# A fill on GpSimd behind every gather of token rows in an embedding and MLP kernel

## Chip, cores and metric

The kernel runs on one core of a Trainium2 chip. The metric is the device time of one execution in microseconds (us); the median of three runs is given, with the lowest and the highest. A profile is one further execution, recorded by the hardware profiler.

The engines are called as in the profile: PE is TensorE (PEld its weight loads), DVE is VectorE, ACT is ScalarE, POOL is GpSimd, and SP is the engine that issues the plain DMAs.

## Reference

A recommendation model over 16384 rows. Every row has 32 token indices into a table of 50000 x 300, three lists of 20 indices into tables of 1000, 5000 and 10000 rows of 64, and four single indices into small tables. The lists are averaged, everything is concatenated to 748 columns, and an MLP of three layers follows. A "wide" sum of one scalar per looked-up index is added before the sigmoid.

```python
tok = word_emb[token_idx].mean(axis=1)                 # (B, 32) -> (B, 300)
e1 = emb_mh1[mh1_idx].mean(axis=1)                     # (B, 20) -> (B, 64); e2, e3 alike
o1 = emb_oh1[oh1_idx]                                  # (B,) -> (B, 64); o2, o3, o4 alike
emb = jnp.concatenate([tok, e1, e2, e3, o1, o2, o3, o4], axis=1)
wide = (wide_mh1[mh1_idx].sum(axis=(1, 2)) + ... + wide_oh4[oh4_idx][:, 0])[:, None]
h = jax.nn.relu(emb @ W1 + b1)                         # 1024
h = jax.nn.relu(h @ W2 + b2)                           # 512
h = jax.nn.relu(h @ W3 + b3)                           # 256
return jax.nn.sigmoid(h @ Wd + bd + wide)
```

## The kernel before

The 16384 rows are cut into 128 tiles of 128 rows. Four tiles make a block for the MLP (the last block is cut into 2, 1 and 1 tiles). Two kinds of lookup run side by side.

**The small tables** are held on the chip, split into three bf16 terms (`terms`). For a tile, one-hot rows are made on VectorE (`one_hots`, L280), TensorE multiplies them into counts (`counts`, L298), ScalarE copies the counts out of PSUM as fp8 (L305), and TensorE multiplies counts by `terms` to get the sums of embeddings (`small_sums`, L323), which VectorE reduces into the tile's row of features `g` (L330).

**The token rows** come from memory. `tokens` walks over the 32 tokens of a tile in 16 groups of two. For each group it takes a buffer `tok_rows` of 128 x 600 floats from a pool of six (`2 * TOK_LAG`), and GpSimd issues two indirect DMAs (L212), each of which fetches one row of 300 floats for each of the 128 partitions. There are 128 x 32 = 4096 such gathers in all. The group is then put on a list, `under_way`. Only when more than three groups are on it (`TOK_LAG`) is the oldest added up by VectorE in `add_up`: the two halves of the buffer into each other (L202), and that into `g` (L203); the first group of a tile goes straight into `g` (L200). A buffer is free for a new gather once L203 (or L200) has read it.

The order on every engine is the order in which the program is written out by hand (`manual_schedule`). The main loop takes each tile in 11 steps. A step issues the one-hots of the next step, the counts of this one, some groups of gathers and additions, some of the small sums of the tile before, and some matmuls of the MLP of the block before. The last three are generators under `Paced`, which hands out their work evenly: 16 token groups over the 11 steps of a tile, so one or two groups in a step. In VectorE's queue, the additions of a step stand behind its one-hots and ahead of those of the following step.

The MLP runs in fp32 on TensorE (L376), with ScalarE applying bias and ReLU (L385). Features are transposed on TensorE (L366) and scaled into `x` by VectorE (L367).

GpSimd has nothing to do but the gathers, apart from seven small instructions at the start: four fills of one column (L518), a fill of 128 x 128 floats for the identity matrix (masks.py:197), a select on it, and an iota.

Of the kernel before, what the change touches and what calls it, by code (L numbers as in the profile page):

```python
# [8 lines left out]
F32 = mybir.dt.float32  # L9
# [8 lines left out]
P = 128  # L18
# [3 lines left out]
D1, D2, D3 = 1024, 512, 256  # L22
TOK_GROUP = 2
TOK_LAG = 3
BLOCK = 512
HALF = P // 2
N_SMALL = 3 * N_MH + 4
# [17 lines left out]
def kernel(  # L45
# [21 lines left out]
    nc = tc.nc  # L67
    B = out.shape[0]
    NSUB = BLOCK // P
    M1, M2, M3 = D1 // P, D2 // P, D3 // P  # L70
# [9 lines left out]

    tokp = ctx.enter_context(tc.tile_pool(name="tok", bufs=2 * TOK_LAG))
    const = ctx.enter_context(tc.tile_pool(name="const", bufs=1))
# [110 lines left out]
            nc.sync.dma_start(out=sb, in_=dram)  # L193

    under_way = []

    def add_up(rows, g, first):
        a, b, n = rows[:, 0:TOK_D], rows[:, TOK_D : 2 * TOK_D], TOK_D
        if first:
            nc.vector.tensor_add(g[:, 0:n], a, b)  # L200
        else:
            nc.vector.tensor_add(a, a, b)  # L202
            nc.vector.tensor_add(g[:, 0:n], g[:, 0:n], a)  # L203

    def tokens(g, it):


        for q in range(N_TOK // TOK_GROUP):
            rows = tokp.tile([P, TOK_GROUP * TOK_D], F32, name="tok_rows")
            for t in range(TOK_GROUP):  # L210
                j = q * TOK_GROUP + t
                nc.gpsimd.indirect_dma_start(  # L212
                    out=rows[:, t * TOK_D : (t + 1) * TOK_D],
                    out_offset=None,
                    in_=word,
                    in_offset=bass.IndirectOffsetOnAxis(ap=it[:, j : j + 1], axis=0),
                )
            under_way.append((rows, g, q))
            if len(under_way) > TOK_LAG:
                rows, to, old_q = under_way.pop(0)  # L220
                add_up(rows, to, old_q == 0)
            yield 1
# [5 lines left out]
    def load_indices(blk):  # L228


        b0 = blk * BLOCK
        it = idxp.tile([P, NSUB, N_TOK], I32, name="it")
        nc.sync.dma_start(
            out=it, in_=idx[b0 : b0 + BLOCK, 0:N_TOK].rearrange("(s p) c -> p s c", p=P)
        )
# [122 lines left out]
    def transposed(gs):  # L358

        n = len(gs) * P  # L360
        x = xp.tile([P, NK, BLOCK], F32, name="x", tag="even")
        for k in range(NK):
            kk = chunk_k[k]
            pt = ps_h.tile([P, BLOCK], F32, name="pt", tag="ph")
            for s, g in enumerate(gs):
# [6 lines left out]
    def layer(dst, weights, bias, src, kks, n_out, n):  # L372
        for m in range(n_out):
            ph = ps_h.tile([P, BLOCK], F32, name="ph", tag="ph")
            for k, kk in enumerate(kks):
# [68 lines left out]
    for t in range(tiles + 1):  # L444
# [4 lines left out]
        if t < tiles:  # L449
            if s == 0 and t:  # L450
                it, sc = next_it, next_sc
            g = gp.tile([P, G_COLS], F32, name="g")
            cnt = cp.tile([P, 2, HALF, n_h], FP8, name="cnt", tag="counts")
            toks = Paced(tokens(g, it[:, s, :].bitcast(U32)), N_TOK // TOK_GROUP, STEPS)
        else:
            last_tokens()
# [76 lines left out]
```

## Time and profile before

| | |
|---|---|
| runs | 5517.34 us median of 3 (5515.67 to 5519.1) |
| profiled execution | 7368.99 us, its span 7367.2 us |
| mean granted TensorE clock, profiled execution | 0.891 |
| PE busy | 5894.3 us (80% of the span) |
| POOL busy | 4079.8 us (55%) |
| DVE busy | 3606.2 us (49%) |
| ACT busy | 2632.3 us (36%) |
| gathers L212 | 4096 of 996 ns |
| DMA, share of 16 engines | 31.1% for the gathers, 629.41 MB |

The busy times belong to the profiled execution and are shares of its span, which is 1.34 times the median of the runs. A busy time counts the records of instructions alone: time in which an engine prepares its next instruction is not in it, and appears as idle time with the releaser "issue". Where a wait is listed, the line reads: engine and line that waited, arrow, engine and line that ended the wait, then us in total, times, and the longest in us. In a timeline, a line reads: start in us, duration in us, engine, line, operation, output and inputs, and in brackets the idle time before it and what ended that.

### The profile page before, as it was taken

What the parts mean: (1) busy time and instruction counts of PE and PEld (TensorE: products, weight loads), DVE (VectorE), ACT (ScalarE), POOL (GpSimd) and SP (SyncE); (2) the same over time, 40 slices, a digit from 0 to 9 for tenths busy, and PEclk for the clock granted to TensorE, in tenths of its full rate; (3) what the DMA queues carried; (4) which work ended last, traced back from release to release, by engine and by line L of the source; (5) the groups of instructions that cost most, each with busy time, mean ns of one, the idle gap of its engine ahead of it and who ended that gap; (6) DMA issues with size and microseconds to landing.
All of it is one profiled execution on the core that took longest, in us unless ns stands there. A gap on an engine that the chain in (4) does not pass through costs nothing.

```text
span 7367.2 us, 103052 instructions
## 1 busy us (share of the span) xinstructions
PE 5894.3 (80%) x41320; PEld 3527.7 (48%) x41320; DVE 3606.2 (49%) x8013; ACT 2632.3 (36%) x3408; POOL 4079.8 (55%) x4103
## 2 busy tenths in 40 slices
PE   3688788878778888878888888888888788888789
PEld 2444444444444444444444444444444444444457
DVE  5544454445454454445444544454445454545443
ACT  4333333333333333333333333333333333333333
POOL 5555555555555555555555555555555555555552
PEclk8789888899898998889888889888988898888999
DMA  5333333333333333333333333333333333333331
GB/s 138 89 90 91 87 87 88 87 90 85 89 86 90 90 88 90 86 89 86 93 86 88 87 90 91 87 87 89 89 89 89 86 90 90 86 91 87 90 87 45
DMA packets 245345, 652.52 MB, mean 89 GB/s; under 512 B 108978, under 2 KB 111989, under 8 KB 244864
## 3 DMA queue, kind: packets, MB, share of 16 engines
q0 software_dynamic: 196608, 629.41, 31.1%
q1 hardware_dynamic: 48255, 16.53, 1.0%
q8 instruction: 323, 5.29, 0.3%
q14 instruction: 159, 1.29, 0.1%
HBM read 645.59 MB, written 0.07 MB: 88 GB/s over the span
## 4 chain that ended last, share of the span: by engine, by line
PE 52%; another core or an unknown queue 26%; ACT 13%; issue 5%; DVE 3%; POOL 0%; DMA 0%; DVEq 0%; SPq 0%; ACTq 0%; POOLq 0%
PE ph L376 24%; PE pg L323 17%; ACT cnt L305 12%; PE pc L298 9%; ACT h L385 1%; PE pt L366 1%; DVE x L367 1%; PE po L399 1%; DVE g L330 0%; PE po L403 0%; DVE slice L280 0%; DVE tok_rows L202 0%; DVE g L203 0%; ACT terms L166 0%
## 5 line engine op out<-in xcount | busy, mean ns | idle before, releaser
L212 POOL DMA_INDIRECT tok_rows<-in_word_emb_dram,it x4096 | 4078.9, 996 | 3207.7 <-DVE g L203 2195.9
L305 ACT ACTIVATE cnt<-pc 128x828 fp8e3<-128x828 f32 (+1 forms) x2816 | 2224.6, 842 | 3325.2 <-PE pc L298 1393.4
L323 PE MATMUL pg<-terms,cnt 128*128 128x195 bf16 x17664 | 2135.3, 271 | 272.0 <-issue 257.2
L280 DVE TENSOR_TENSOR row<-iota,sc 128x768 bf16<-128x768 bf16 (+1 forms) x1408 | 764.7, 543 | 2673.5 <-remote 1282.8
L323 PEld LDWEIGHTS <-cnt 128*128 128x128 fp8e3 x17664 | 1759.2, 147 | 502.7 <-issue 363.6
L298 PE MATMUL pc<-slice,row 64*128 64x138 bf16 x16384 | 880.2, 232 | 1047.6 <-ACT cnt L305 883.0
L376 PE MATMUL ph<-x,w_sb 128*128 128x512 f32 (+5 forms) x3264 | 1625.2, 626 | 43.7 <-issue 41.5
L298 PEld LDWEIGHTS <-row 64*128 64x128 bf16 x16384 | 570.1, 97 | 2182.3 <-issue 1611.2
L376 PE MATMUL ph<-h,w_sb 128*128 128x512 f32 (+2 forms) x2720 | 1404.9, 645 | 26.5 <-issue 24.7
L203 DVE TENSOR_TENSOR g<-g,tok_rows 128x300 f32<-128x300 f32 x1920 | 904.6, 471 | 65.6
L202 DVE TENSOR_TENSOR tok_rows<-tok_rows 128x300 f32<-128x300 f32 x1920 | 890.4, 464 | 0.0
L376 PEld LDWEIGHTS ph<-x,w_sb 128*128 128x128 f32 (+1 forms) x3264 | 610.5, 211 | 516.7 <-issue 505.3
L280 DVE TENSOR_TENSOR slice<-iota,sc 128x828 bf16<-128x828 bf16 (+1 forms) x1408 | 803.8, 571 | 0.0
L385 ACT ACTIVATE h<-ph,b_sb 128x512 f32<-128x512 f32 (+2 forms) x476 | 315.4, 663 | 1225.4 <-remote 739.8
L376 PEld LDWEIGHTS ph<-h,w_sb 128*128 128x128 f32 x2720 | 524.4, 217 | 422.9 <-issue 420.5
L330 DVE TENSOR_REDUCE g<-pg 128x130 f32<-128x390 f32 (+1 forms) x512 | 249.8, 509 | 827.9 <-remote 392.0
L367 DVE TENSOR_SCALAR x<-pt,scale 128x512 f32<-128x512 f32 (+4 forms) x204 | 140.9, 717 | 111.1 <-PE pt L366 104.4
L366 PE MATMUL pt<-ident,g 128*128 128x128 f32 (+1 forms) x768 | 124.8, 292 | 51.8 <-DVE x L367 51.4
L366 PEld LDWEIGHTS pt<-ident,g 128*128 128x128 f32 (+1 forms) x768 | 84.5, 143 | 91.7 <-DVE x L367 83.8
L305 ACT ACT_TABLE_LOAD x32 | 41.1, 1283 | 145.8 <-PE pc L298 145.0
L399 PE MATMUL po<-h,wd_sb 128*1 128x512 f32 (+2 forms) x136 | 62.0, 573 | 0.6 <-issue 0.3
L200 DVE TENSOR_TENSOR g<-tok_rows 128x300 f32<-128x300 f32 x128 | 59.2, 463 | 0.0
(32 smaller groups left out, 346.4 us busy)
## 6 DMA issues: line engine op xcount, KB each, us to landing
tok_rows<-in_word_emb_dram,it POOLq DMA_INDIRECT x4096
ix<-in_idx_dram SPq DMA_DIRECT2D x128, 32.0 KB
w_sb<-in_W_dram SPq DMA_DIRECT2D x6, 512.0 KB
it<-in_idx_dram SPq DMA_DIRECT2D x32, 64.0 KB
w_sb<-in_W_dram SPq DMA_DIRECT2D x1, 2048.0 KB
raw<-in_mh_dram SPq DMA_DIRECT2D x1, 975.0 KB
out_dram<-h SPq DMA_DIRECT2D x31, 2.0 KB
raw<-in_mh_dram SPq DMA_DIRECT2D x1, 292.5 KB
```

Source lines behind the costliest of these rows:

```text
L202: nc.vector.tensor_add(a, a, b)
L203: nc.vector.tensor_add(g[:, 0:n], g[:, 0:n], a)
L212: nc.gpsimd.indirect_dma_start(out=rows[:, t * TOK_D : (t + 1) * TOK_D], out_offset=None, in_=word, in_offset=bass.IndirectOffsetOnAxis(ap ...
L280: nc.vector.tensor_tensor(one[:, 0:rows, :].rearrange("p i (n d) -> p i n d", d=2), iota[:, 0:n].rearrange("p (n d) -> p n d", d=2).unsque ...
L298: nc.tensor.matmul(pc[:, f, k * n_h : (k + 1) * n_h], hot[0][half, k0 + k, :], hot[1][half, k0 + k, :], start=True, stop=True,)
L305: nc.scalar.activation(cnt[:, :, b + k0 : b + k0 + n, :].rearrange("l f k h -> l f (k h)"), pc[:, :, 0 : n * n_h], AF.Copy, scale=0.5, sat ...
L323: nc.tensor.matmul(pg[:, j, :], by_slice[:, :, h], terms[:, h, :], start=(h == h0), stop=(h == h1 - 1))
L330: nc.vector.tensor_reduce(g[:, at : at + n * ROW].rearrange("p (f d) -> p f d", f=n), pg[:, 0:n, :].rearrange("p f (c d) -> p f d c", c=3) ...
L366: nc.tensor.transpose(pt[:kk, s * P : (s + 1) * P], chunk(g, k), ident)
L367: nc.vector.tensor_scalar(x[:kk, k, 0:n], pt[:kk, 0:n], scale[:kk, k : k + 1], None, ALU.mult)
L376: nc.tensor.matmul(ph[:, 0:n], weights[:kk, k, m * P : (m + 1) * P], src[:kk, k, 0:n], start=(k == 0), stop=(k == len(kks) - 1),)
L385: nc.scalar.activation(dst[:, m, 0:n], ph[:, 0:n], AF.Relu, bias=bias[:, m : m + 1])
```

## The change

A tile `pause` of 128 x 128 floats is added, and after each gather GpSimd fills it with zeros. Nothing reads `pause`. There are 4096 fills, all in GpSimd's own queue.

```diff
+PAUSE = 128
...
     under_way = []
+    pause = const.tile([P, PAUSE], F32, name="pause")
...
     def tokens(g, it):
...
                     in_=word,
                     in_offset=bass.IndirectOffsetOnAxis(ap=it[:, j : j + 1], axis=0),
                 )
+                nc.gpsimd.memset(pause, 0.0)
             under_way.append((rows, g, q))
```

## Prediction

> **What bounds the kernel now.** I read the times first, then the page's chain (part 4), then the waits, then GpSimd's own groups and timeline. The runs take 5517.34 us (median of three, 5515.67 to 5519.1); the profiled execution took 7368.99, a span of 7367.2 with 1.8 around it. It is a third slower than the runs, so I ask first what it has that they may lack. The chain answers:
>
> ```profile
> PE 52%; another core or an unknown queue 26%; ACT 13%; issue 5%; DVE 3%; POOL 0%; DMA 0%; DVEq 0%; SPq 0%; ACTq 0%; POOLq 0%
> ```
>
> A kernel on one core has no other core to wait for. Listed in order of time, these pieces are stalls of mostly 9.2 us, 26.2% in all (26% above): 0.262 x 7367.2 = 1930 us. Without them 5437 us are left, close to the runs. I take the stalls for the recording's, and the runs for an execution with few of them. That is an inference.
>
> POOL (GpSimd) has 0% of the chain, and the waits make it look idle:
>
> ```profile
> POOL tok_rows L212 <- DVE g L203: 2195.9, 1064, 9.8
> ...
> POOL tok_rows L212 <- issue: 876.6, 2827, 2.1
> ```
>
> A gather waits until the addition of L203 frees its buffer, 2195.9 us in all; nobody in the list waits for gathered rows. Read alone, this says that GpSimd has room. But the second line is no slack: 876.6 / 2827 = 0.31 us is lost ahead of gathers that waited for nothing. The timeline of POOL, where gathers run unhindered, shows the same:
>
> ```profile
> 2001.87 0.95 POOL L212 DMA_INDIRECT tok_rows<-in_word_emb_dram,it  x1 [0.30 <-DVE g L203]
> 2003.12 0.95 POOL L212 DMA_INDIRECT tok_rows<-in_word_emb_dram,it  x1 [0.30 <-issue]
> 2004.37 0.95 POOL L212 DMA_INDIRECT tok_rows<-in_word_emb_dram,it  x1 [0.30 <-issue]
> 2005.63 0.95 POOL L212 DMA_INDIRECT tok_rows<-in_word_emb_dram,it  x1 [0.30 <-issue]
> ```
>
> Starts are 1.25 us apart, not 0.95: each gather costs its record plus 0.30. The first line shows that 0.30 also when DVE is named as releaser. The groups of POOL, shapes apart:
>
> ```profile
> L212 POOL DMA_INDIRECT tok_rows<-in_word_emb_dram,it x4096 | 4078.9, 996 | 3207.7 <-DVE g L203 2195.9 <-issue 876.6 <-DVE g L200 64.8
> ...
> masks.py:197 POOL MEMSET ident<- 128x128 f32 x1 | 0.2, 205 | 0.3 <-POOLq L518 0.3
> ...
> L518 POOL MEMSET const-float32-0.0<- 128x1 f32 x1 | 0.1, 99 | 0.2 <-issue 0.2
> ```
>
> The mean gather is 0.996 us; with a gap of 0.305 (between the 0.30 and the 0.31 above) GpSimd needs 1.301 us per gather and 4096 x 1.301 = 5329 us. Gathers begin 3.0 us into the span and the last starts at 7287.1, 80 before its end: 5329 + 83 = 5412 us is the least that GpSimd allows. In the profiled execution that is 73% of the span; in the runs it would be 98%. TensorE stands as near: 5894.3 us busy at a mean granted clock of 0.891 is 5252 us at full clock. **Two engines, both a few per cent under 5517**: that is my reading.
>
> **What the Trainium skill says.** "Perfetto Trace Analysis", section GPSIMD Engine Instruction, calls GpSimd's recorded spans unreliable and would have one time by the spacing of starts; the trace agrees (0.95 recorded, 1.25 apart). "GPSIMD Engine Reference", 3.1, gives 1.03 cycles per element at 1.2 GHz for simple bodies, 110 ns for 128 columns by my estimate; the trace agrees (205 - 99 = 106 ns between the two fills above). The same page, 2.1, says that one GpSimd instruction doesn't hold the next back until it has completed; the trace agrees for fills, since four one-column ones at the start begin about 28 ns apart (0.25, 0.28, 0.30, 0.33 us) while each records 99 to 119 ns. "SBUF — State Buffer", Who interferes with whom, says that a VectorE operation with two inputs in SBUF contends with GpSimd instructions that read SBUF, not with those that only write it; no row here shows a fill beside VectorE.
>
> **The change part by part.** Nothing is removed and nothing moved; no DMA and no queue on SP is touched. 4096 fills are added to GpSimd's queue, one after each gather, all to one tile that nobody reads, so no other engine waits for a fill. Behind a fill stand the next gather of the pair, and the next pair.
>
> - *One fill.* The same operation on the same shape (128x128 f32) records 205 ns: one price, if the next gather starts only when the fill has been written. The other is its throughput, 28 ns of issue + 106 ns for the columns = 134 ns, if the write's tail overlaps what follows. I take the middle, 0.17 us. The outer ends are 0 (it fits inside the 0.305 us between gathers) and 0.51 (205 ns plus a second gap of 0.305).
> - *The sum on GpSimd.* 4096 x 0.17 = 696 us. 4096 x (1.301 + 0.17) = 6025, and with 83 at the ends **6108 us**. With 0.134 it is 5961, with 0.205 it is 6252.
> - *What covers it.* In the profiled execution, the 2195.9 us of waits for L203; there 6108 still fits under 7367.2, and I expect its span to grow little, to between 7370 and 7600. In the runs the cover is only 5517 - 5412 = 105 us, or 0.026 us per gather; of 696 us, 591 stick out.
> - *What is late next.* `add_up` stands in VectorE's queue ahead of the next step's one-hots (L280). When gathered rows come late, L200 or L202 waits for the DMA, L280 behind them, then the count matmuls (L298), ScalarE's copies (L305) and the other matmuls behind those on TensorE. The six buffers let GpSimd run some groups ahead, which smooths bursts but adds nothing to a rate that is too low everywhere: a tile of 128 rows takes 5517 / 128 = 43.1 us now and would need 32 x 1.471 = 47.1 us of GpSimd.
> - *The extra tile* takes 512 bytes per partition of SBUF: no time.
>
> **Rivals.**
> 1. *The fill is hidden* (not slower). If the 0.305 us between gathers is preparation of the next gather, and the fill runs meanwhile, it costs up to 0.026 us and the bound isn't reached: 5517, within a few us. For it: the gap is constant and nothing that the profile shows fills it. Against it: the gap may be spent by the very cores that would run the fill. It decides below (5517 - 83) / 4096 - 1.301 = 0.026 us per fill. A slight gain is possible if spaced gathers disturb others less.
> 2. *The gather is shorter in the runs than in the profile.* The record's minimum spacing is 1.245; with 1.25 and 0.134 the sum is 4096 x 1.384 + 83 = 5752. For it: the recording lengthens other things. Against it: a denser execution has VectorE busier, and gathers beside VectorE's additions last 1.12 us and not 0.95 (2000.45, while L202 runs).
> 3. *A fill breaks the gathers apart* and brings a dispatch gap of its own: 0.51 us, 4096 x 1.811 + 83 = 7501. For it: the gap stands before every gather. Against it: the small fills at the start have none between them. Half of that extra is 6870.
> 4. *The fill isn't executed* because nothing reads the tile: 5517. Nothing in the diff suggests that.
>
> **How the numbers follow.** Main case (GpSimd sets the pace, a fill costs 0.134 to 0.205): 0.55, 5961 to 6252, with 6108 the forecast. Rival 2: 0.15. Rival 3, whole or in part (above 6400): 0.15. Rivals 1 and 4: 0.15, of which 0.09 within 0.2% (11 us, about what a measurement of this kernel can tell from no change), 0.05 faster, 0.01 slower. So slower is 0.86. The range is 5650 to 6650: below it lie rivals 1 and 4, above it the worse half of rival 3, about 0.2 together.
>
> **What would show it.** In the profile after: 4096 MEMSETs on POOL writing `pause`, some 205 ns each; starts of gathers that wait for nothing 1.42 to 1.5 us apart and not 1.25 (the number that decides, whatever the span does); POOL's wait for L203 fallen from 2195.9 us by several hundred; first waits of L202 or L200 for the DMA of `tok_rows`. The forecast is wrong if the starts stay 1.25 apart (rival 1), if they are 1.7 or more (rival 3), or if they widen to about 1.47 and the runs stay near 5517: then a gather takes less in the runs, at most 5434 / 4096 - 0.17 = 1.157 us.

## The result

The changed kernel takes **5877.12 us** (median of 4 runs, 5873.89 to 5882.95) against 5517.34 before (5515.67 to 5519.1): **1.0653 times, 95% interval 1.0635 to 1.0672**. The forecast was 6108 in a range of 5650 to 6650. Its profiled execution took 5882.95 us, a span of 5881.1, as long as the other runs.

One thing is needed to read the numbers below. The chips used here differ: on two of them, as in the runs of the result, the kernel before takes about 5520 us, on another it takes 7220 in every run, and the profile shown ahead of the prediction, with its 7369, has the same pattern as the runs there (which chip it was taken on is not known). So I profiled the kernel before again (run e5): on a chip where it takes 5527 the profile is undisturbed. Below, "before" is that profile, and ratios on the 7220 chip are to its own times of before.

The chain of the profile after (part 4 of the page):

```profile
POOL 43%; DMA 29%; DVE 12%; issue 8%; PE 7%; POOLq 0%; ACT 0%; SPq 0%; DVEq 0%; ACTq 0%
```

GpSimd and the landing of its gathers hold 72% of it, TensorE 7%. The waits of the profile after (engine and line, what ended the wait, us in total, times, longest):

```profile
ACT cnt L309 <- PE pc L302: 2277.3, 1158, 8.8
DVE tok_rows L204 <- DMA tok_rows<-in_word_emb_dram,it: 1735.7, 1321, 4.3
...
POOL tok_rows L215 <- DVE g L205: 186.5, 861, 9.9
```

The added lines move the line numbers: L204 is the former L202, L205 is L203, L215 is L212, L284 is L280, L302 is L298 and L309 is L305. VectorE waits 1735.7 us for gathered rows; GpSimd waits 186.5 us for buffers. The groups and then the timeline of POOL after:

```profile
L215 POOL DMA_INDIRECT tok_rows<-in_word_emb_dram,it x4096 | 4131.5, 1009 | 767.8 <-issue 551.7 <-DVE g L205 186.5 <-DVE g L202 14.3
L221 POOL MEMSET pause<- 128x128 f32 x4096 | 908.8, 222 | 2.4
```

```profile
2003.93 0.95 POOL L215 DMA_INDIRECT tok_rows<-in_word_emb_dram,it  x1 [0.17 <-DVE g L205]
2004.88 0.22 POOL L221 MEMSET pause<- 128x128 f32 x1
2005.27 0.95 POOL L215 DMA_INDIRECT tok_rows<-in_word_emb_dram,it  x1 [0.16 <-issue]
```

The fill begins the moment the gather's record ends and takes 222 ns. The next gather begins 0.16 to 0.17 us after the fill, where without a fill it begins 0.30 after the gather. Starts are 1.34 us apart: 0.22 us of fill make the step only 0.09 longer.

### The profile page after: what moved, and what is told of

Read it like the earlier page. It is cut to its first block, busy times and chain, and to the rows that moved or that the text cites. A ratio compares the mean times of both kernels' runs of the same rounds, so it can differ in the third digit from the quotient of the medians.

```text
span 5881.1 us, 107148 instructions
## 1 busy us (share of the span) xinstructions
PE 5269.5 (90%) x41320; PEld 3225.2 (55%) x41320; DVE 3674.5 (62%) x8013; ACT 2637.4 (45%) x3408; POOL 5032.7 (86%) x8199
## 4 chain that ended last, share of the span: by engine, by line
POOL 43%; DMA 29%; DVE 12%; issue 8%; PE 7%; POOLq 0%; ACT 0%; SPq 0%; DVEq 0%; ACTq 0%
POOL tok_rows L215 35%; DMA tok_rows<-in_word_emb_dram,it 28%; POOL pause L221 8%; DVE tok_rows L204 5%; DVE g L205 5%; PE ph L380 3%; PE pg L327 2%; PE po L403 1%; DVE x L371 1%; PE pt L370 1%; PE pc L302 1%; DVE g L334 0%; POOLq L215 0%; DVE slice L284 0%; DMA raw<-in_mh_dram 0%
## 5 line engine op out<-in xcount | busy, mean ns | idle before, releaser
L215 POOL DMA_INDIRECT tok_rows<-in_word_emb_dram,it x4096 | 4131.5, 1009 | 767.8 <-issue 551.7
L309 ACT ACTIVATE cnt<-pc 128x828 fp8e3<-128x828 f32 (+1 forms) x2816 | 2208.9, 838 | 2344.4 <-PE pc L302 2277.3
L327 PE MATMUL pg<-terms,cnt 128*128 128x195 bf16 x17664 | 1888.3, 258 | 149.8 <-DVE g L334 149.7
L204 DVE TENSOR_TENSOR tok_rows<-tok_rows 128x300 f32<-128x300 f32 x1920 | 906.7, 472 | 1752.6 <-DMA tok_rows<-in_word_emb_dram,it 1735.7
L327 PEld LDWEIGHTS <-cnt 128*128 128x128 fp8e3 x17664 | 1628.6, 145 | 307.7 <-issue 154.2
L380 PE MATMUL ph<-x,w_sb 128*128 128x512 f32 (+5 forms) x3264 | 1484.8, 583 | 0.0
L302 PEld LDWEIGHTS <-row 64*128 64x128 bf16 x16384 | 508.4, 96 | 1383.1 <-DVE slice L284 632.5
L380 PE MATMUL ph<-h,w_sb 128*128 128x512 f32 (+2 forms) x2720 | 1263.9, 592 | 0.0
L302 PE MATMUL pc<-slice,row 64*128 64x138 bf16 x16384 | 770.9, 226 | 346.8 <-DVE slice L284 307.6
L205 DVE TENSOR_TENSOR g<-g,tok_rows 128x300 f32<-128x300 f32 x1920 | 904.6, 471 | 65.8
L221 POOL MEMSET pause<- 128x128 f32 x4096 | 908.8, 222 | 2.4
L284 DVE TENSOR_TENSOR row<-iota,sc 128x768 bf16<-128x768 bf16 (+1 forms) x1408 | 758.7, 539 | 143.1 <-PE pc L302 142.6
L284 DVE TENSOR_TENSOR slice<-iota,sc 128x828 bf16<-128x828 bf16 (+1 forms) x1408 | 801.6, 569 | 0.0
L380 PEld LDWEIGHTS ph<-x,w_sb 128*128 128x128 f32 (+1 forms) x3264 | 561.6, 194 | 389.4 <-issue 377.3
L380 PEld LDWEIGHTS ph<-h,w_sb 128*128 128x128 f32 x2720 | 473.6, 197 | 320.3 <-issue 318.2
L202 DVE TENSOR_TENSOR g<-tok_rows 128x300 f32<-128x300 f32 x128 | 60.1, 470 | 39.4 <-DMA tok_rows<-in_word_emb_dram,it 39.2
```

The lines of the kernel that those rows point to most:

```text
L215: nc.gpsimd.indirect_dma_start(out=rows[:, t * TOK_D : (t + 1) * TOK_D], out_offset=None, in_=word, in_offset=bass.IndirectOffsetOnAxis(ap ...
L221: nc.gpsimd.memset(pause, 0.0)
L284: nc.vector.tensor_tensor(one[:, 0:rows, :].rearrange("p i (n d) -> p i n d", d=2), iota[:, 0:n].rearrange("p (n d) -> p n d", d=2).unsque ...
L302: nc.tensor.matmul(pc[:, f, k * n_h : (k + 1) * n_h], hot[0][half, k0 + k, :], hot[1][half, k0 + k, :], start=True, stop=True,)
L309: nc.scalar.activation(cnt[:, :, b + k0 : b + k0 + n, :].rearrange("l f k h -> l f (k h)"), pc[:, :, 0 : n * n_h], AF.Copy, scale=0.5, sat ...
L327: nc.tensor.matmul(pg[:, j, :], by_slice[:, :, h], terms[:, h, :], start=(h == h0), stop=(h == h1 - 1))
```

## The experiments

Three explanations for how the gap behaves, by the letters in the expectations: S, everything follows in line; F, the 0.305 us is a floor counted from the gather's end, beside which a fill runs free until it is too long; C, each fill costs a fixed amount. Two for who set the pace before: B, GpSimd; T, TensorE.

**e5 and e6: before and after, once more.** No edit.

> The kernel before, unchanged, profiled once more. In the profile of before and on the chip of the four runs above, matmuls whose records lie close together are completed some 8 us late about 200 times in an execution, and ScalarE's copies wait for them; in the profile after that is nearly absent. If this chip lets TensorE run without such halts (a time near 5517), theory B (GpSimd sets the pace of before) expects the waits of the profile after: L202 and L200 waiting for the rows by 1000 us or more in all, POOL and the gathers on the chain, gathers about 1.33 us apart on the mean. Theory T (TensorE sets it) expects matmuls on the chain and POOL waiting for L203 by some 100 us or more beyond that of the profile after (186 us). If it takes about 7200 here as well, the halts belong to before on this chip too.

> The changed kernel, unchanged, beside before on this chip. Where before takes about 5517: 5877 again (1.0635 to 1.0672 times). Where before takes about 7220 because TensorE halts: if the halts come with dense matmul work, slower gathers thin that work out and the changed kernel is the faster one there, 5880 to 6700; if the halts have nothing to do with how dense the work is, it is slower there too, 7250 or more.

e5, one execution, took 5523.16 us, e6 5881.65 (1.0643 times before, 1.0625 to 1.0661). The chain of e5, two of its waits, and its gathers:

```profile
PE 26%; DMA 24%; issue 19%; DVE 17%; POOL 13%; ACT 0%; SPq 0%; DVEq 0%; POOLq 0%; ACTq 0%
```

```profile
DVE tok_rows L202 <- DMA tok_rows<-in_word_emb_dram,it: 1299.0, 1129, 4.3
...
POOL tok_rows L212 <- DVE g L203: 176.2, 402, 10.0
```

```profile
L212 POOL DMA_INDIRECT tok_rows<-in_word_emb_dram,it x4096 | 4120.5, 1006 | 1319.7 <-issue 807.1 <-DVE tok_rows L202 199.7 <-DVE g L203 176.2
```

VectorE waits 1299.0 us for rows where the disturbed profile had no such line, and GpSimd's wait for L203 is 176.2 us and not 2195.9. Of GpSimd's 1319.7 us of idle time, 4096 x 0.304 = 1245 is the gap after every gather; 75 us are real waits. The 4095 steps from first gather to last take 5438 us, 1.328 each, 98% of the span. GpSimd is full in this execution, as B says. TensorE still has 26% of the chain, and this profile alone doesn't say whether it holds the pace as well; e7 and e9 do.

**e7: fewer gathers.** This is an edit of the kernel before. TensorE's work stays; the last six of the 32 tokens are left out of the sum.

```diff
+USED_TOK = 26
-        for q in range(N_TOK // TOK_GROUP):
+        for q in range(USED_TOK // TOK_GROUP):
-            toks = Paced(tokens(...), N_TOK // TOK_GROUP, STEPS)
+            toks = Paced(tokens(...), USED_TOK // TOK_GROUP, STEPS)
```

> The kernel before without any fill, and without the last six of the 32 tokens: 13 groups of gathers in a tile and not 16 (3328 gathers and not 4096); TensorE's and ScalarE's work is untouched. Theory B (GpSimd's 1.328 us per gather set the 5517): GpSimd now needs 3328 x 1.328 + 83 = 4503, so the time falls to what TensorE needs, whose busy time in the clean profile of before is 5167: 5200 to 5400. Theory T (TensorE set the 5517): 5500 to 5520, no change, as GpSimd had room already.

5275.12 us, 0.9561 times before (0.9545 to 0.9577). The chain and GpSimd's longest wait of e7 (L213 and L204 are the former L212 and L203):

```profile
PE 91%; DVE 5%; DMA 1%; issue 1%; ACT 1%; POOL 0%; DVEq 0%; SPq 0%; ACTq 0%; POOLq 0%
```

```profile
POOL tok_rows L213 <- DVE g L204: 950.2, 646, 10.2
```

Now TensorE has 91% and GpSimd waits 950.2 us for buffers. T falls: with its work untouched the kernel is 244 us faster. TensorE's floor is about 5275, which is 4% below before. The edit also takes away six in 32 of VectorE's additions and of the gathered bytes, so e7 alone doesn't single out GpSimd; e11, which adds work to VectorE, and the fills on GpSimd, which move no gathered bytes, do.

**e9: half of the fills.** This and the next three edit the changed kernel.

```diff
-                nc.gpsimd.memset(pause, 0.0)
+                if t == TOK_GROUP - 1:
+                    nc.gpsimd.memset(pause, 0.0)
```

> A fill of 128 columns after the second gather of each pair alone (2048 fills); tried above on a chip on which before takes 7220. Where before takes about 5517: theory B (GpSimd paced the kernel before already, each fill costs 0.088 us) 5697, 5680 to 5720; rival T (105 us of room were there, the rest spread over the fills) 5644 or less.

5703.35 us, 1.0331 times (1.0314 to 1.0348): 186 us for 2048 fills, 0.091 us each; the 4096 of the change cost 360 us, 0.088 each. Within the intervals the cost is the same for the first half of the fills as for all of them, with no room to use up first, as B says. The timeline of POOL in e9 has both gaps side by side:

```profile
2000.79 0.22 POOL L222 MEMSET pause<- 128x128 f32 x1
2001.17 1.01 POOL L215 DMA_INDIRECT tok_rows<-in_word_emb_dram,it  x1 [0.17 <-issue]
2002.49 0.95 POOL L215 DMA_INDIRECT tok_rows<-in_word_emb_dram,it  x1 [0.30 <-issue]
```

**e8: a fill of one column.**

```diff
-PAUSE = 128
+PAUSE = 1
```

> The fill covers 1 column; tried above on a chip on which the kernel before takes 7220, where its gathers started 1.253 us apart at the median of all, against 1.25 without a fill. Theory F (the gap of 0.305 us after a gather is a floor, beside which a short fill runs free): where before takes about 5517, this takes 5517 to 5545. Theory S (everything follows in line, gap 0.165): below 5500. Rival C (a fixed cost per fill): 5877.

5560.26 us, 1.0077 times (1.0061 to 1.0094). The timeline of POOL in e8:

```profile
2002.30 0.95 POOL L215 DMA_INDIRECT tok_rows<-in_word_emb_dram,it  x1 [0.19 <-issue]
2003.24 0.12 POOL L221 MEMSET pause<- 128x1 f32 x1
2003.55 0.96 POOL L215 DMA_INDIRECT tok_rows<-in_word_emb_dram,it  x1 [0.19 <-issue]
```

The fill takes 0.12 us and the gap behind it is 0.19: from one gather's end to the next gather the same 0.305 as with no fill, and gathers that wait for nothing start 1.25 us apart as before. S asked for 0.12 + 0.165 = 0.28, C for 5877; both fall. F holds for the spacing. The time is still 41 us over before, above F's 5545. GpSimd doesn't wait longer for buffers than in e5. What is new is a pause of about 1 us beyond the usual gap, behind the fill and ahead of every 106th gather; the profile shows nothing that ends it. One of them:

```profile
1995.76 0.12 POOL L221 MEMSET pause<- 128x1 f32 x1
1997.21 1.01 POOL L215 DMA_INDIRECT tok_rows<-in_word_emb_dram,it  x1 [1.33 <-issue]
```

The trace of e8 has 37 of them, some 40 us in all, and its gathers are 10 us shorter in sum than those of e5: the 30 us that are left are the difference of the two profiled executions. The profile after has 37 such pauses too (34 us) and e10 has 35; e5, e9 and e12 have none. What they are stays open.

**e10: 256 columns.** `PAUSE = 256`.

> The fill covers 256 columns; tried above where before takes 7220, where its gathers started 1.447 us apart at the median and not 1.339. Where before takes about 5517: the step's growth of 0.107 us over 128 columns makes 5877 + 4096 x 0.107 = 6315 (6280 to 6350); if TensorE or VectorE hid some of it, less.

6343.68 us, 1.1484 times (1.1465 to 1.1503). Groups of POOL in e10:

```profile
L215 POOL DMA_INDIRECT tok_rows<-in_word_emb_dram,it x4096 | 4182.8, 1021 | 748.1 <-issue 648.8 <-DVE g L205 43.7 <-DVE wide L345 14.7
L221 POOL MEMSET pause<- 128x256 f32 x4096 | 1345.5, 328 | 2.0
```

The forecast range of 6280 to 6350 holds. The time grew by 467 us over the changed kernel, 0.114 a step: the fill grew from 222 to 328 ns, the gap behind it stayed at 0.16 to 0.17, the gathers are 12 ns longer (1021, not 1009), and the other waits some 5 ns shorter. From 128 to 256 columns, every nanosecond of fill is paid.

**e11: the fills on VectorE.**

```diff
-                nc.gpsimd.memset(pause, 0.0)
+                nc.vector.memset(pause, 0.0)
```

> The same 4096 fills of 128 columns on VectorE; tried above where before takes 7220 (7439 there, 165 ns a fill). They stand in VectorE's queue ahead of the additions, whose buffers GpSimd has to get back, and VectorE waits for rows by some 1300 us in the clean profile of before. If only GpSimd's rate counts, these waits cover 4096 x 0.165 = 676 us of fills: 5517 to 5560. Rival (any instruction added to the loop from gather to addition to next gather costs its length): 5517 + 676 = 6190.

5461.34 us, **0.989 times before (0.9874 to 0.9907)**: 1.1% faster, which neither side expected. Groups of POOL, one of VectorE, and VectorE's wait for rows in e11:

```profile
L215 POOL DMA_INDIRECT tok_rows<-in_word_emb_dram,it x4096 | 4063.6, 992 | 1326.4 <-issue 839.5 <-DVE pause L221 190.9 <-DVE tok_rows L204 143.9
```

```profile
L221 DVE MEMSET pause<- 128x128 f32 x4096 | 675.8, 165 | 190.9
```

```profile
DVE tok_rows L204 <- DMA tok_rows<-in_word_emb_dram,it: 627.5, 791, 3.8
```

The wait for rows is 627.5 us and not 1299.0: the 676 us of added VectorE work lie almost wholly inside it. And the gather's record fell from 1006 to 992 ns: 4096 x 0.014 = 57 us, about the gain of 56. So the gain is in the gathers themselves. In the trace of e5, the 381 gathers whose record overlaps no VectorE instruction last 949 ns on average, and 302 beside L202 alone last 948; but 378 that meet all of `slice` of L280, L202 and L203 last 1167. That the fills on VectorE spread its operations so that fewer gathers meet several of them is my explanation. The trace of e11 agrees in part: 314 gathers meet all three there, and 913 gathers, not 1287, last over 1 us. No run changes that spread by itself, so the cause is not shown.

**e12: a seventh buffer for gathered rows**, in the kernel before.

```diff
-    tokp = ctx.enter_context(tc.tile_pool(name="tok", bufs=2 * TOK_LAG))
+    tokp = ctx.enter_context(tc.tile_pool(name="tok", bufs=2 * TOK_LAG + 1))
```

> The kernel before without any fill, with seven buffers for gathered rows and not six. In the clean profile of before, 4095 steps of the gathers take 5438 us, of which 1.006 + 0.304 us each is gather and gap: 5365; the other 73 us are waits for buffers. Theory B: a seventh buffer can win back only these: 5445 to 5517. A rival in which buffers, not GpSimd's rate, set the pace (a loop of six buffers from gather to addition and back): a sixth less of the step, down to TensorE's floor of about 5275.

5517.65 us, 0.9997 times (0.9988 to 1.0005): nothing. Buffers did not set the pace, and not even the 73 us came back: in e5's trace nearly all of these waits, some 68 us, lie in the first 100 and the last 200 us.

**e1 to e4, on the chip where before takes 7220.31 us** (7198.8 to 7249.47): the kernels of e8, e10, e9 and e11.

> The fill after each gather covers 1 column and not 128. Theory S (GpSimd sets the pace before and after; gather, fill and a start-up gap of 0.165 us follow one another, the gap having been 0.305 without a fill): a one-column fill should record about 0.115 us (0.222 less 127 columns at 0.83 ns), so a step is about 0.115 + 0.165 = 0.28 us beyond the gather, 0.02 less than the 0.305 of before: 5517 - 80 to 5517. Theory F (the gap of 0.305 is a floor, counted from the end of the gather, beside which a fill of up to 0.14 us runs free): starts 1.25 us apart, 5517 within 11. Rival C (every fill costs a fixed 0.088 us for the interruption, whatever its size): 5877.

> The fill after each gather covers 256 columns and not 128. Theories S and F alike: 128 more columns at 0.83 ns are 0.107 us more per gather, all of it in GpSimd's step; starts 1.45 us apart at the least, 5877 + 4096 x 0.107 = 6315 (6250 to 6350). Rival C (fixed cost per fill): 5877. A rival in which other engines still hide part of the step: between 5877 and 6200.

> A fill of 128 columns after the second gather of each pair alone, 2048 fills and not 4096. Theory B (GpSimd paced the kernel before already, so every fill costs 0.088 us from the first one on): 5517 + 2048 x 0.088 = 5697. Rival T (TensorE set 5517, and GpSimd had the 105 us of room that the prediction gave it; then 360 us beyond it mean 0.1135 us per fill): 5517 + 2048 x 0.1135 - 105 = 5644.

> The same 4096 fills of 128 columns, issued in the same places of the program, but on VectorE. If it is GpSimd's rate that counts, VectorE has the room (3675 us busy; 4096 fills of some 0.2 us make about 4500 of 5517) and only the later handover of buffers and one-hots is felt: 5517 to 5600. Rival: any added instruction in the chain gathers to additions to one-hots costs its length: 5517 + 4096 x 0.09 or more, 5880 and above.

7254.79, 6356.43, 7097.76 and 7438.61 us: 1.0047 (1.0036 to 1.0058), **0.8796** (0.8766 to 0.8826), 0.9822 (0.9787 to 0.9858) and 1.031 (1.0275 to 1.0346) times before there. None of the expected times applied. The waits of e1, then of e2, say what is different:

```profile
DVE row L284 <- remote: 1563.5, 291, 10.9
...
ACT cnt L309 <- remote: 1379.3, 378, 10.6
```

```profile
ACT cnt L309 <- PE pc L302: 2218.8, 1010, 9.3
DVE tok_rows L204 <- DMA tok_rows<-in_word_emb_dram,it: 2095.8, 1511, 4.0
```

"Remote" is a wait that ended with no record near it. In the trace, TensorE starts the count matmuls at their usual time, and the semaphore that they raise comes up to 8 us late. Stretches of over 6.5 us without it: 219 in the profile ahead of the prediction, 179 in e1, 131 in e3, 236 in e4, 13 in e2, 6 in e5, in e6 and in the profile after. e2's waits have the pattern of the undisturbed chips, and its time is near that of e10. That slower gathers thin out TensorE's work and so nearly end the halts is my reading, which no run isolates. Why that chip halts is open, and the changed kernel itself was not run on it. What of e1 to e4 holds everywhere is GpSimd's own spacing: medians of 1.254 us in e1 and 1.447 in e2, as in e8 and e10 (1.252 and 1.445).

## Why the prediction was right, and where it was off

*The bound.* Right that GpSimd's gathers, 0% of the chain shown, set the pace in the runs (e5, e7, e9), and right that a gather costs record plus gap. The reading "two engines, both a few per cent under 5517" was too cautious: GpSimd was at 5517, TensorE 244 us below.

*The stalls.* Right to set 1930 us aside, wrong on the cause: they are not the recording's. Profiles of e5 and after run at the speed of the other runs, and on one chip every run of this kernel takes the longer time.

*The step of 1.301 us*, the first mis-sized term. In undisturbed executions it is 1.328: gathers last 1.006 us beside a busier VectorE, not 0.996, the gap is 0.304, and 0.018 are waits. With these GpSimd needed 5521 and not 5412; without them it would be 5449, but the fills and a seventh buffer left the waits (e9, e12). **The 105 us of cover didn't exist** (e9).

*The fill of 0.17 us*, the second: it cost 0.088. So 5877 lies under the main case's 5961 to 6252, and the number that was to decide, starts of 1.42 to 1.5 us, came out as 1.34. The record of a fill is 0.222 us, near the first price (0.205), but the gap ahead of the next gather shrank from 0.305 to 0.164. Both bracket ends, 0.134 and 0.205, treated fill and gap as separate; in fact 0.14 us of the gap can run beside a fill. Rival 1 had this mechanism and held it to be all or nothing. Of 0.222 us, 0.222 + 0.164 - 0.305 = 0.081 is left; longer gathers (0.003) and the pauses described under e8 (34 us, 0.008 each) come on top, and the waits at the ends are a little shorter.

*The sum.* The two errors have opposite signs: 6108 - 4096 x (0.17 - 0.088) + 105 = 5877. (This comes out by construction, as 0.088 and 105 are taken from the measured times.) That the miss was 231 us and not 336 is luck, the second error taking back part of the first. The range held because it was wide enough for its rivals: what set the pace was right, and the price of the fill was about twice what it cost.

*Rivals 2 and 3.* The gather is longer in the runs than assumed, not shorter; no second dispatch gap appears. Rival 4 falls with 4096 fills in the profile.

*What is late next.* As forecast, L204 waits for rows, but these waits were there before: 1735.7 us after, 1299.0 in e5. The one-hots and counts behind it are later too (the weight loads of L302 wait 632.5 us for `slice` of L284, against 337.1 in e5). The fall of GpSimd's wait for L203 by several hundred us, told for the disturbed profile, is no evidence: 2195.9 there, but 176.2 in e5 and 186.5 after. The forecast span of 7370 to 7600 failed with its premise.

*The pages of the Trainium skill.* Spacing of starts was the right measure ("Perfetto Trace Analysis", GPSIMD Engine Instruction). The 1.03 cycles per element of "GPSIMD Engine Reference", 3.1, at 1.2 GHz 0.86 ns by estimate, held nearly: 118, 222 and 328 ns for 1, 128 and 256 columns are 0.82 to 0.83 ns per column. "SBUF — State Buffer", Who interferes with whom, expects two-input VectorE operations to hinder GpSimd's reads; the 1167 against 949 ns of e5's gathers agree with that, the 948 ns beside L202 alone, which has two inputs too, do not.

## What to carry to other kernels

An engine that issues gathers is full when its record plus its gap fills the time, whatever its busy share says: here 75% busy was 98% of the time. Before a wait in one profile is read as room, look whether that execution has the speed of the runs; if not, rebuild the engine's need from spacing times count. And a small instruction added behind a gather cost, in this kernel, what sticks out of the gap: at one column nothing but the rare pauses, four tenths of its length at 128, and all of the further length up to 256.

## What was not expected

- Fills on VectorE instead of GpSimd make the kernel 1.1% faster than before (5461 us), through gathers of 992 instead of 1006 ns.
- 0.305 us pass between two gathers whether a one-column fill runs in it or not; after fills of 128 and 256 columns the next gather follows in 0.164.
- With a fill behind every gather GpSimd pauses for about 1 us at every 106th gather (e8, e10 and the changed kernel); with a fill behind every second one it doesn't (e9).
- On one chip TensorE's results come up to 8 us late some 200 times in an execution, at a mean granted clock of 0.90 (e1) against 0.985 (e5); fills of 256 columns on GpSimd took that to 13 times and the time from 7220 to 6356 us.
